# The tail of a filter stage: earlier loads into an idle buffer, and the last chunk's stores on ScalarE's queue

## The chip, the cores and the metric

One core of a Trainium2 chip runs the kernel as one launch. The metric is the time of an execution on the device in microseconds (us), the median over runs. The profile is of one such execution; its span, from the first instruction to the last, is 1531.3 us.

## The reference, cut to what matters

The input is x, eight images of 32 x 32 pixels with 128 channels, so eight sequences of T = 1024 tokens. Three blocks follow one another, each added to the stream: attention over each image, a pair of state-space mixers (one forwards, one backwards), and a spectral filter unit. The change lies in the last one:

```
t = t + _L1_ffn_ref(_ln_t(t), sigma, phi, M_u, M_phi_plus, M_phi_minus, ...)
# _L1_ffn_ref, for the bank that a hard choice picks:
#   U_plus, U_minus = causal convolutions of u with 16 filters phi[:, k] (by FFT)
#   out = sum over k of (U_plus[k] @ Mpp[k] + U_minus[k] @ Mpm[k]) * sigma[k]**0.25
#       + three short autoregressive terms u[t - i] @ Mu[i]
```

The output is the sum of this unit and the stream that came in (the residual). Everything is float32.

## The kernel before, in words

`fast_kernel` computes the filter unit in the frequency domain: forward transforms of the tokens (stage f), a 128 x 128 complex matrix for each frequency applied to the spectra (stage g), and the inverse transform with the residual added (stage i). A general path is kept for inputs that the fast one can't take; it does not run here.

**Stage g, lines 1321 to 1423.** There are NF = 128 frequencies in 16 chunks of FC = 8. The loop at L1406 is a software pipeline over chunks, one step ahead: in the pass for chunk c, TensorE makes the matrices of chunk c + 1 (`matrices`, L1336), ScalarE and VectorE copy them into the tile `gs` (L1347, L1349), and TensorE applies the matrices of chunk c to the spectra `u` (`apply`, L1370). `gs` has two buffers of 64 KB in each partition. In the last pass (chunk 15) no further matrices are made, so the buffer of chunk 14 lies idle from the moment that chunk 14's last `apply` ends. After each quarter of a chunk `gather` (L1385 to L1393) combines the products; after every second quarter, SyncE's queue stores `sums` (256 KB) into the DRAM tensor `yd`, so two stores per chunk. `yd` is indexed by frequency first; the following stage needs frequencies in partitions. That turn of the data is why it goes through DRAM.

**Stage i, lines 1425 to 1468.** The output is made in four pieces (k, h): half k of each sequence, and images h*4 to h*4 + 3. A piece needs its spectra `yt` with the frequency in the partition: two loads (i = 0, 1, the real and imaginary part) of 128 rows x 4 images x 2 KB, 1024 KB each, and its residual `res` from the DRAM tensor `xa`, 1024 KB. VectorE forms `z` from them (four operations, L1444), TensorE multiplies with the inverse transform `inv` (eight matmuls, four outputs of 128 x 512, L1449; the profile shows each float32 matmul as two records), VectorE adds the residual (four operations, L1456), and ScalarE's queue stores the piece, 1024 KB (L1459).

The first piece's spectra live in a tile of their own, `early_yt`, that is filled during stage g: after each chunk, `fetch` (L1397 to L1401) loads the eight rows of the chunk before it, two loads of 64 KB (8 rows x 8 KB). The other three pieces have their `yt` in a pool of two buffers and are loaded whole, after the last chunk. `res` has three buffers, so the fourth residual waits for the first piece's store.

**What sets the order.** TensorE, VectorE, ScalarE and GpSimd execute in the order in which the source is written. The DMAs of SyncE are placed by a scheduler, but each queue then issues strictly in its order: a DMA whose wait is not met holds back everything behind it on that queue. DMAs take eight completion semaphores in turn, and one that takes a semaphore first waits for the DMA that had it before. In effect, a DMA waits for the one eight places ahead of it in the joint order of both queues.

Of the kernel before, what the change touches and what calls it, by code (L numbers as in the profile page):

```python
# [8 lines left out]
F32 = mybir.dt.float32  # L9
AF = mybir.ActivationFunctionType  # L10
ALU = mybir.AluOpType
AX = mybir.AxisListType
PSUM = bass.MemoryType.PSUM

P = 128
B = 8
T = 1024
NT = T // P
C = 128
# [11 lines left out]
NB = 2  # L31
NF = 128
FC = 8
# [11 lines left out]
def fast_kernel(ctx: ExitStack, tc: tile.TileContext, a: dict, out: bass.AP, bad: bass.AP):  # L45
    nc = tc.nc
    x = a["x"]
# [27 lines left out]
    me = dram.tile([P, 2 * KF, P], F32, name="me")  # L75

    ud = dram.tile([NF // FC, P, B, NB, 2, 4, FC], F32, name="ud")
    yd = dram.tile([NF, NB, B, 2, 4, C], F32, name="yd")

    def filled(name, shape, value):  # L80
        t = ctile(shape, name)
# [436 lines left out]
    with ExitStack() as s:  # L518
# [87 lines left out]
        sums = {}  # L606
# [608 lines left out]
    with ExitStack() as s:  # L1215
# [105 lines left out]
        with ExitStack() as s2:  # L1321
# [56 lines left out]
            def gather(c, n, turn, py):  # L1378

                if turn == 0:  # L1380
                    gathered["sums"] = p3.tile([P, 4, C], F32, tag="sums", name=f"sums{c}_{n}")
                    gathered["both"] = p2.tile([P, 2, C], F32, tag="both", name=f"both{c}_{n}")
                sums, both = gathered["sums"], gathered["both"]
                half = p2.tile([P, C], F32, tag="half", name=f"half{c}_{n}_{turn}")
                nc.scalar.copy(half, py[:, 1, :])  # L1385
                nc.vector.tensor_tensor(both[:, turn, :], py[:, 0, :], half, ALU.add)
                nc.vector.tensor_tensor(sums[:, 2 + turn, :], py[:, 0, :], half, ALU.subtract)
                if turn == 0:
                    return
                nc.vector.tensor_tensor(sums[:, 0, :], both[:, 0, :], both[:, 1, :], ALU.add)  # L1390
                nc.vector.tensor_tensor(sums[:, 1, :], both[:, 0, :], both[:, 1, :], ALU.subtract)
                at = c * FC + n * 4
                nc.sync.dma_start(  # L1393
                    yd[at : at + 4].rearrange("f k b i q e -> (f k b i) (q e)"), sums.rearrange("p q e -> p (q e)")
                )

            def fetch(c):  # L1397

                rows = slice(c * FC, (c + 1) * FC)
                for i in range(2):  # L1400
                    nc.sync.dma_start(early_yt[rows, i], yd[rows, 0, 0:4, i])  # L1401

            chunks = NF // FC
            gs, us, gathered = {}, {}, {}
            s2.enter_context(tc.manual_schedule(engines=IN_ORDER))
            for c in range(-1, chunks):  # L1406
# [13 lines left out]
                        gather(c, half, turn, py)  # L1420
                if c > 0:
                    fetch(c - 1)
            fetch(chunks - 1)

        with ExitStack() as s2:
            p2 = s2.enter_context(tc.tile_pool(name="i_2", bufs=2))
            p3 = s2.enter_context(tc.tile_pool(name="i_3", bufs=3))
            ps_o = s2.enter_context(tc.tile_pool(name="i_ps_o", bufs=4, space=PSUM))

            def loaded(k, h):  # L1430

                yt = early_yt
                if k or h:
                    yt = p2.tile([P, 2, 4, 4, C], F32, tag="yt", name=f"yt{k}_{h}")
                    for i in range(2):
                        nc.sync.dma_start(yt[:, i], yd[:, k, h * 4 : h * 4 + 4, i])
                res = p3.tile([P, 4, 4, C], F32, tag="res", name=f"res{k}_{h}")
                nc.sync.dma_start(res, xa[h * 4 : h * 4 + 4, :, NB - 1 - k].rearrange("b p r c -> p b (r c)"))
                return yt, res

            def back(k, h, yt, res):
                z = p2.tile([P, 2, 2, 4, C], F32, tag="z", name=f"z{k}_{h}")
                for r, i, op in ((0, 0, ALU.subtract), (0, 1, ALU.add), (1, 0, ALU.add), (1, 1, ALU.subtract)):
                    nc.vector.tensor_tensor(z[:, r, i], yt[:, i, :, 2, :], yt[:, 1 - i, :, 3, :], op)  # L1444
                blk = NB - 1 - k
                for r in (0, 2, 1, 3):
                    po = ps_o.tile([P, 4, C], F32, tag="o", name=f"pz{k}_{h}_{r}")
                    for i in range(2):
                        nc.tensor.matmul(  # L1449
                            po,  # L1450
                            lhsT=inv[:, r, i, :],
                            rhs=z[:, r // 2, i] if r % 2 else yt[:, i, :, r // 2, :],
                            start=(i == 0),
                            stop=(i == 1),
                        )
                    nc.vector.scalar_tensor_tensor(  # L1456
                        res[:, :, r, :], po, keep[:, blk : blk + 1], res[:, :, r, :], ALU.mult, ALU.add
                    )
                nc.scalar.dma_start(  # L1459
                    out[h * 4 : h * 4 + 4, blk * 512 : (blk + 1) * 512].rearrange("b (p r) c -> p b (r c)", r=4), res  # L1460
                )

            pieces = [(k, h) for k in range(NB) for h in range(2)]
            got = [loaded(*piece) for piece in pieces[:3]]
            for n, piece in enumerate(pieces):
                back(*piece, *got[n])
                if n + 3 < len(pieces):
                    got.append(loaded(*pieces[n + 3]))


@with_exitstack
# [803 lines left out]
```

## Time and profile before

| what | value |
|---|---|
| time, median of 3 runs | 1534.85 us (1531.8 to 1535.4) |
| span of the profiled execution | 1531.3 us |
| busy: TensorE, VectorE, ScalarE, GpSimd | 1438.4, 1152.8, 867.8, 442.4 us |
| mean TensorE clock granted | 0.979 |
| DMA, mean over the span | 58 GB/s (89.05 MB) |
| last chunk's last matmul ends | 1478.9 us |
| first matmul of the inverse transform | 1488.3 us |
| last store of the output issued | 1523.6 us |

The profile gives busy times of the engines, a timeline, the waits with what ended them, and for any stretch the granted clock, the share of time that the 16 DMA engines were busy, and the GB/s that they moved. TensorE is busy for 94% of the span, but that says little on the end of the kernel: the last 52 us, after the last chunk, have a rhythm of their own, and the change touches only these and the few us ahead of them. A name such as SPq or ACTq is the queue of SyncE or ScalarE, where a DMA is issued; the time beside it is that of the issue, not of the transfer.

### The profile page before, as it was taken

How to read it: one execution, taken by the hardware profiler on the slowest of the kernel's cores; microseconds unless marked ns; L12 is line 12 of the kernel's file. 1: busy time of each engine (PE TensorE's matmuls, PEld its weight loads, DVE VectorE, ACT ScalarE, POOL GpSimd, SP SyncE). 2: the span in 40 equal slices, each digit the busy share in tenths (PEclk: the TensorE clock that was granted, in tenths of full speed). 3: DMA queues.
4: the chain of work that ended last, by engine and by line, in shares of the span. 5: the costliest groups of instructions: out<-in, count | busy, mean ns of one | idle time of the engine just before them, and what ended most of it. 6: DMA issues, size and time to landing. Idle time of an engine off the chain costs nothing.

```text
span 1531.3 us, 45713 instructions
## 1 busy us (share of the span) xinstructions
PE 1438.4 (94%) x20118; PEld 879.1 (57%) x20118; DVE 1152.8 (75%) x2314; ACT 867.8 (57%) x1228; POOL 442.4 (29%) x488
## 2 busy tenths in 40 slices
PE   5999999999998899999999999999779999999976
PEld 2323333333334566666665666666569899989962
DVE  6689888778675888888888888887655577777744
ACT  3756666666666465656566666555345455555520
POOL 2336786584201112121111112111166411111100
PEclk9999999999999899999999999999899999999989
DMA  7001111110000011010101010101047622322258
GB/s 187 21 1 35 49 35 37 47 42 8 1 1 13 2 26 31 15 42 15 42 15 42 15 42 15 42 15 42 14 152 219 182 69 70 79 75 74 66 143 304
DMA packets 131960, 89.05 MB, mean 58 GB/s; under 512 B 41480, under 2 KB 114824, under 8 KB 131752
## 3 DMA queue, kind: packets, MB, share of 16 engines
q1 hardware_dynamic: 129640, 81.84, 19.4%
q8 instruction: 160, 2.62, 0.8%
q10 hardware_dynamic: 2112, 4.19, 0.7%
q14 instruction: 48, 0.39, 0.1%
HBM read 44.60 MB, written 33.55 MB: 51 GB/s over the span
## 4 chain that ended last, share of the span: by engine, by line
PE 83%; DVE 5%; ACT 5%; issue 3%; DMA 2%; POOL 1%; ACTq 0%; DVEq 0%; SPq 0%; POOLq 0%
PE pg L1336 9%; PE pt L618 9%; PE py L1370 8%; PE pb L847 7%; PE po L639 7%; PE pd L659 4%; PE sy L1042 4%; PE pz L798 4%; PE pp L798 4%; PE pl L935 4%; PE spo L1072 3%; PE pe L953 3%; PE sb L905 2%; PE pst L973 2%; PE pf L1254 2%
## 5 line engine op out<-in xcount | busy, mean ns | idle before, releaser
L623 ACT ACTIVATE pr<-pt 128x1024 f32<-128x1024 f32 x256 | 248.1, 1021 | 115.1 <-PE pt L618 113.5
L648 DVE TENSOR_TENSOR two<-pr,pr 128x1024 f32<-128x1024 f32 x128 | 162.9, 1314 | 19.5 <-ACT pr L623 18.6
L1349 ACT COPY gs<-pg 128x512 f32<-128x512 f32 x256 | 133.8, 598 | 63.8 <-PE pg L1336 48.8
L1347 DVE COPY gs<-pg 128x512 f32<-128x512 f32 x256 | 159.2, 685 | 13.5 <-PE pg L1336 10.1
L618 PE MATMUL pt<-q,k 32*128 32x512 f32 x1024 | 159.8, 654 | 7.0 <-ACT pr L623 4.5
L1336 PE MATMUL pg<-taps,mst 32*128 32x128 f32 x4096 | 147.5, 280 | 4.8 <-ACT gs L1349 2.2
L1336 PEld LDWEIGHTS pg<-taps,mst 32*128 32x128 f32 x4096 | 134.4, 186 | 18.1 <-issue 13.8
L639 PE MATMUL po<-pr,v 128*32 128x512 f32 x1024 | 140.2, 605 | 0.0
L827 DVE SCALAR_TENSOR_TENSOR xs<-xp,cw,xs 128x1024 f32<-128x1024 f32 x96 | 123.1, 1283 | 7.4 <-ACT xs L819 5.2
L1370 PE MATMUL py<-gs,u 128*32 128x128 f32 (+1 forms) x4096 | 127.8, 277 | 0.0
L1370 PEld LDWEIGHTS py<-gs,u 128*32 128x32 f32 (+1 forms) x4096 | 112.0, 141 | 7.3
L1102 POOL TENSOR_TENSOR rms<-rms_v,mhalf 128x8 f32<-128x8 f32 x16 | 39.2, 2452 | 262.2 <-DVE rms_v L1100 262.2
L847 PE MATMUL pb<-bxt,wbc 128*128 128x512 f32 x256 | 114.2, 598 | 0.3 <-ACT zs L838 0.3
L781 POOL TENSOR_TENSOR dau<-upto,da 128x2048 f32<-128x2048 f32 x16 | 57.9, 3619 | 133.7 <-DVE state L987 133.7
L618 PEld LDWEIGHTS pt<-q,k 32*128 32x128 f32 x1024 | 47.6, 186 | 84.9 <-issue 33.0
L1359 POOL TENSOR_SCALAR u<-u 128x512 f32<-128x512 f32 x16 | 24.1, 1504 | 229.0 <-PE pg L1336 117.7
L990 DVE SCALAR_TENSOR_TENSOR state<-state,dec,pst 128x64 f32<-128x64 f32 x448 | 87.3, 275 | 1.1
L847 PEld LDWEIGHTS pb<-bxt,wbc 128*128 128x128 f32 x256 | 47.1, 189 | 56.0 <-issue 53.8
L639 PEld LDWEIGHTS po<-pr,v 128*32 128x32 f32 x1024 | 28.0, 109 | 88.4 <-issue 84.4
L1042 PEld LDWEIGHTS sy<-lm,xdt 64*64 64x64 f32 x2048 | 58.8, 137 | 29.9 <-DVE ec L1016 15.2
L659 PE MATMUL pd<-two,ones 128*32 128x512 f32 x512 | 73.3, 613 | 0.2
L1042 PE MATMUL sy<-lm,xdt 64*64 64x64 f32 x2048 | 65.5, 226 | 5.5 <-DVE lm L1012 5.5
(272 smaller groups left out, 2846.2 us busy)
## 6 DMA issues: line engine op xcount, KB each, us to landing
ud<-sp SPq DMA_DIRECT2D x8, 1024.0 KB
u<-ud SPq DMA_DIRECT2D x32, 256.0 KB
yd<-sums SPq DMA_DIRECT2D x32, 256.0 KB
moved<-state SPq DMA_DIRECT2D x48, 128.0 KB
yt<-yd SPq DMA_DIRECT2D x6, 1024.0 KB
X<-in_x SPq DMA_DIRECT2D x8, 512.0 KB
part_p<-in_L_ffn_M_phi_plus SPq DMA_DIRECT2D x32, 128.0 KB
part_m<-in_L_ffn_M_phi_minus SPq DMA_DIRECT2D x32, 128.0 KB
```

The costliest lines, as they stand in the source:

```text
L618: nc.tensor.matmul(pt[:, i, :], lhsT=k[rows, j * P : (j + 1) * P], rhs=q[rows, cols], start=True, stop=True)
L623: nc.scalar.activation(pr[:, 2 * g : 2 * g + 2, :].rearrange("p i t -> p (i t)"), pt.rearrange("p i t -> p (i t)"), AF.Exp, scale=SCALE,)
L639: nc.tensor.matmul(po[rows, :], lhsT=vs[b][:, j, rows], rhs=pr[:, h, :], start=(j == 0), stop=(j == NT - 1))
L648: nc.vector.tensor_tensor(two, sums["pr"][:, 2 * g : 2 * g + 2, :], pr[:, 2 * g : 2 * g + 2, :], ALU.add)
L659: nc.tensor.matmul(sums["d"][(2 * g + i) * DH : (2 * g + i + 1) * DH, :], lhsT=ones[:, :DH], rhs=two[:, i, :], start=(j == 1), stop=(j == ...
L827: nc.vector.scalar_tensor_tensor(acc, xp[:, at : at + T], cw[u.d][:, n, i : i + 1], acc, ALU.mult, ALU.add)
L847: nc.tensor.matmul(u.pb[:, i * 512 : (i + 1) * 512], lhsT=wbc[u.d][:, k, :], rhs=xt[:, at : at + 512], start=(k == 0), stop=(k == KC - 1),)
L1042: nc.tensor.matmul(u.py[c][h * HP : (h + 1) * HP, r, j, :], lhsT=left, rhs=right, start=(kind == 0), stop=(kind == 1 or k is None),)
L1336: nc.tensor.matmul(pts[g][:, e, :], lhsT=mst[rows, n * 4 + e, :], rhs=taps[rows, cols].rearrange("p f q m i -> p (f q m i)"), start=True, ...
L1347: nc.vector.tensor_copy(to, frm)
L1349: nc.scalar.copy(to, frm)
L1370: nc.tensor.matmul(py[t * 32 : t * 32 + 32 - 16 * m, q // 2, :], lhsT=u[:, i, m:, :, :, q * FC + f].rearrange("p k b i -> p (k b i)"), rhs ...
```

## The change

It is meant to use the time of the last chunk for the loads of stage i. Almost all rows of `yd` are known by then, and one `gs` buffer is idle.

- The two tensors part: `yd` keeps chunks 0 to 14, and a new DRAM tensor `yl` takes chunk 15. The two stores into `yl` are issued by ScalarE's queue.
- At the end of the pass for chunk 14 the idle `gs` buffer becomes a tile `free` of eight slots of 8 KB in each partition. Six hold the spectra of the second, third and fourth piece, two hold the residuals of the first and second. For each of the six spectra slots SyncE loads rows 0 to 111 (chunks 0 to 13, 896 KB) and rows 112 to 119 (chunk 14, 64 KB) as two DMAs.
- After the last chunk, ScalarE's queue loads rows 120 to 127 of all four pieces from `yl`: eight DMAs of 64 KB.
- When chunk 15's matrices are used up, their buffer becomes a second `free`: two slots for the residuals of the third and fourth piece, two for `z`. No buffer has to be waited for after that.
- Stage i uses the eight PSUM buffers of stage g in place of four of its own, and `z` of the following piece is computed between the two halves of a piece.
- `fetch` stays as it was for chunks 0 to 14: the call for chunk 14 stands in the pass for chunk 15, and so, in the source, after the new loads.

```
-    yd = dram.tile([NF, NB, B, 2, 4, C], F32, name="yd")
+    yd = dram.tile([NF - FC, NB, B, 2, 4, C], F32, name="yd")
+    yl = dram.tile([FC, NB, B, 2, 4, C], F32, name="yl")
...
+                to = yd[at : at + 4] if c + 1 < chunks else yl[n * 4 : n * 4 + 4]
+                (nc.sync if c + 1 < chunks else nc.scalar).dma_start(
+                    to.rearrange("f k b i q e -> (f k b i) (q e)"), sums.rearrange("p q e -> p (q e)")
+                )
+            old, last = (slice(0, NF - 2 * FC), slice(NF - 2 * FC, NF - FC)), slice(NF - FC, NF)
+            def free():
+                t = p2.tile([P, P, C], F32, tag="gs", name="free")
...
                 if c > 0:
                     fetch(c - 1)
-            fetch(chunks - 1)
+                if c == chunks - 2:
+                    room = free()
...
+                    for n in range(4):
+                        k, h = pieces[n]
+                        for i in range(2):
+                            if n:
+                                for rows in old:
+                                    nc.sync.dma_start(yts[n][i][rows], yd[rows, k, h * 4 : h * 4 + 4, i])
+                        if n < 2:
+                            load_residual(k, h, results[n])
+            for n, (k, h) in enumerate(pieces):
+                for i in range(2):
+                    nc.scalar.dma_start(yts[n][i][last], yl[:, k, h * 4 : h * 4 + 4, i])
+            room = free()
+            for n in range(2):
+                results.append(half_piece(room, n))
+                load_residual(*pieces[2 + n], results[2 + n])
+            zs = [half_piece(room, 2 + n).rearrange("p (r i) b c -> p r i b c", r=2) for n in range(2)]
...
+            z = turned_back(0)
+            for n, (k, h) in enumerate(pieces):
+                for r in (0, 2):
+                    back(n, r, z)
+                following = turned_back(n + 1) if n + 1 < len(pieces) else None
+                for r in (1, 3):
+                    back(n, r, z)
+                z = following
```

More of the change, by code (lines that the diff above doesn't have):

```diff
@@ L1392, in gather, with half_piece, load_residual @@
                 at = c * FC + n * 4
+                to = yd[at : at + 4] if c + 1 < chunks else yl[n * 4 : n * 4 + 4]
+                (nc.sync if c + 1 < chunks else nc.scalar).dma_start(
+                    to.rearrange("f k b i q e -> (f k b i) (q e)"), sums.rearrange("p q e -> p (q e)")
+                )
+            chunks = NF // FC
+            old, last = (slice(0, NF - 2 * FC), slice(NF - 2 * FC, NF - FC)), slice(NF - FC, NF)
+            def free():
+                t = p2.tile([P, P, C], F32, tag="gs", name="free")
+                return t.rearrange("p n e -> p (n e)").rearrange("p (k x) -> p k x", k=8)
+            def half_piece(t, k):
+                return t[:, k].rearrange("p (b r c) -> p b r c", b=4, r=4)
+            def load_residual(k, h, res):
                 nc.sync.dma_start(
-                    yd[at : at + 4].rearrange("f k b i q e -> (f k b i) (q e)"), sums.rearrange("p q e -> p (q e)")
+                    res.rearrange("p b r c -> p b (r c)"),
+                    xa[h * 4 : h * 4 + 4, :, NB - 1 - k].rearrange("b p r c -> p b (r c)"),
                 )
@@ L1401, in fetch @@
                     nc.sync.dma_start(early_yt[rows, i], yd[rows, 0, 0:4, i])
-            chunks = NF // FC
             gs, us, gathered = {}, {}, {}
@@ L1422, in fast_kernel @@
                     fetch(c - 1)
-            fetch(chunks - 1)
[L1425 to L1442, printed above, removed]
+                if c == chunks - 2:
+                    room = free()
+                    pieces = [(k, h) for k in range(NB) for h in range(2)]
+                    yts = [[early_yt[:, i] for i in range(2)]]
+                    yts += [[half_piece(room, 2 * n + i) for i in range(2)] for n in range(3)]
+                    results = [half_piece(room, 6 + n) for n in range(2)]
+                    for n in range(4):
[6 more added lines that the diff above has]
+                            load_residual(k, h, results[n])
@@ new lines, in fast_kernel, with turned_back @@
+            for n, (k, h) in enumerate(pieces):
[6 more added lines that the diff above has]
+            zs = [half_piece(room, 2 + n).rearrange("p (r i) b c -> p r i b c", r=2) for n in range(2)]
+            def turned_back(n):
+                y, z = yts[n], zs[n % 2]
@@ L1443, in back @@
                 for r, i, op in ((0, 0, ALU.subtract), (0, 1, ALU.add), (1, 0, ALU.add), (1, 1, ALU.subtract)):
-                    nc.vector.tensor_tensor(z[:, r, i], yt[:, i, :, 2, :], yt[:, 1 - i, :, 3, :], op)
+                    nc.vector.tensor_tensor(z[:, r, i], y[i][:, :, 2, :], y[1 - i][:, :, 3, :], op)
+                return z
+            def back(n, r, z):
+                k, h = pieces[n]
                 blk = NB - 1 - k
[L1446 to L1457, printed above, removed]
-                    )
+                po = ps_g.tile([P, 4, C], F32, tag="g", name=f"pz{n}_{r}")
+                for i in range(2):
+                    nc.tensor.matmul(
+                        po,
+                        lhsT=inv[:, r, i, :],
+                        rhs=z[:, r // 2, i] if r % 2 else yts[n][i][:, :, r // 2, :],
+                        start=(i == 0),
+                        stop=(i == 1),
+                    )
+                to = results[n][:, :, r, :]
+                nc.vector.scalar_tensor_tensor(to, po, keep[:, blk : blk + 1], to, ALU.mult, ALU.add)
@@ L1459, in back @@
+            z = turned_back(0)
[6 more added lines that the diff above has]
+                z = following
+                blk = NB - 1 - k
                 nc.scalar.dma_start(
-                    out[h * 4 : h * 4 + 4, blk * 512 : (blk + 1) * 512].rearrange("b (p r) c -> p b (r c)", r=4), res
-                )
@@ L1463, in fast_kernel @@
[L1463 to L1468, printed above, removed]
+                    out[h * 4 : h * 4 + 4, blk * 512 : (blk + 1) * 512].rearrange("b (p r) c -> p b (r c)", r=4),
+                    results[n].rearrange("p b r c -> p b (r c)"),
+                )
```

## The prediction

> **What bounds the kernel now.** I read the timeline of the last 62 us first, then the waits in it, then busy time and DMA by stretch. The timeline:
>
> ```profile
> 1469.78 9.07 PE L1370 MATMUL py<-gs,u 128*32 128x128 f32 x320
> ...
> 1473.12 0.34 SPq L1393 DMA_DIRECT2D yd<-sums  x1
> ...
> 1480.57 0.37 SPq L1438 DMA_DIRECT2D res<-xa  x1
> 1482.22 0.64 SPq L1401 DMA_DIRECT2D early_yt<-yd  x2
> ...
> 1488.27 6.75 PE L1449 MATMUL pz<-early_yt,inv 128*128 128x512 f32 x8 [9.43 <-DMA res<-xa]
> ...
> 1516.39 1.98 PE L1449 MATMUL pz<-yt,inv 128*128 128x512 f32 x4 [2.04 <-DMA yt<-yd]
> ...
> 1523.57 0.38 ACTq L1459 DMA_DIRECT2D out<-res  x1
> ```
>
> The first row holds five times 64 matmuls: chunk 14's last quarter and all of chunk 15. So chunk 14's buffer is idle from about 1469.8 + 9.07/5 = 1471.6, only 7.2 us before the chunks end at 1478.9. From there TensorE waits 9.4 us until 1488.27, for the last eight rows of `early_yt`: the load named as its releaser (`res`) is not among what it needs, `early_yt` is. I call the start of the first piece S; here S = 1488.3. From S to the end it is 1531.3 - 1488.3 = 43.0 us. The waits in the tail:
>
> ```profile
> PE pz L1449 <- DMA res<-xa: 9.4, 1, 9.4
> DVE z L1444 <- DMA early_yt<-yd: 9.1, 1, 9.1
> ...
> DVE res L1456 <- DMA res<-xa: 1.8, 1, 1.8
> ```
>
> What S to the end costs without waits for data: eight half-clock records until the next group starts at 1494.86 take 6.6 us; 56 more at 3.43 us for eight (1494.86 to 1498.29) take 24.0, with 0.2 for the last one to drain; the last addition 0.75 and two short gaps 0.1; from the issue of the last store to the end 1531.3 - 1523.6 = 7.7. Sum 39.3. The measured 43.0 has 3.7 more, the waits for the fourth piece's `yt` and residual. So loads that lie ready would save 3.7 us after S. The rest is decided by S itself, and S by DMA:
>
> ```profile
> 1471.70:1480.60 8.90, 7.15 (x260) 6.85 (x252) 3.65 (x16) 1.34 (x5) 0.00 (x0) 1.00 0.23 77
> 1480.60:1485.50 4.90, 0.00 (x0) 0.00 (x0) 0.00 (x0) 0.00 (x0) 0.00 (x0) 0.87 0.90 293
> 1485.50:1488.50 3.00, 0.23 (x1) 0.26 (x2) 0.00 (x0) 0.00 (x0) 0.00 (x0) 0.50 1.04 110
> 1488.50:1514.00 25.50, 25.30 (x52) 10.59 (x52) 16.05 (x24) 0.00 (x0) 0.00 (x0) 0.88 1.05 395
> ```
>
> The last three columns are TensorE's clock, DMA share and GB/s. While chunk 15 is multiplied DMA is 23% busy; that is the room the change wants. From 1488.5 on DMA is full at 395 GB/s, and computing runs beside it: piece 1 starts when 128 KB have come, the other 9 MB come while it works. The third row is odd: DMA is as busy as ever but moves only 110 GB/s, for 3.0 us. Those are the us in which the two eight-row loads of `early_yt` (128 KB) go through.
>
> [...]after 1503 stores from ScalarE's queue and loads from SyncE's together still make about 400 GB/s. So ScalarE's queue adds no bandwidth. [...]of 3.0 us x 110 GB/s = 330 KB, the pair is 131 KB; the other 199 KB would take 0.5 us at 395, so the pair cost 2.5 us, 1.25 each in place of 0.17 at full rate.
>
> **The change, part by part.** The listing of the changed kernel's order shows where SyncE's queue puts what:
>
> ```
> L1412 free<-xa 128x4x512              residual of piece 1
> L1396 yd<-sums_1 128x512              chunk 14's second store
> L1454 free<-yd 112x4x512, 8x4x512     twice, piece 2
> L1412 free<-xa 128x4x512              residual of piece 2
> L1454 free<-yd 112x4x512, 8x4x512     four times, pieces 3 and 4
> L1421 early_yt<-yd 8x4x512            twice: chunk 14's rows of piece 1
> L1412 free<-xa 128x4x512              twice: residuals of pieces 3 and 4
> ```
>
> This is the point on which all hangs. The rows 112 to 119 of `early_yt` are fetched at 1475.8 and 1477.0 before; now they stand behind every load of pieces 2 to 4, and TensorE and VectorE can't start piece 1 without them. So S is the time at which nearly everything has been loaded, and loads and computing, side by side before, come one after the other.
>
> S, step by step. The first new load can go at 1471.7; before, the store issued at 1480.14 showed traffic 0.9 us later, so data flows from 1472.6. At 395 GB/s, 1024 KB take 2.65 us.
> 1. Wide loads and stores ahead: two residuals 2048 KB, chunk 14's store 256, six loads of 896 KB 5376, two stores of chunk 15 512: 8192 KB, 21.2 us. I take 112 rows at the rate of 128; no row shows them[...].
> 2. Eight-row loads on SyncE's queue: six and the two of `early_yt`, at 1.25 each 10.0 us (1.4 at full rate).
> 3. Eight-row loads on ScalarE's queue: eight; from 0.17 to 1.25 each. [...]I take 0.7, 5.6 us (1.4 to 10).
> 4. From the last data to the waiting engine 0.5 us: the loads that wait for the store of 1480.14 issue at 1482.22, so of these 2.1 us 0.9 are the start, 0.7 its 256 KB, and 0.5 the landing.
>
> S = 1472.6 + 21.2 + 10.0 + 5.6 + 0.5 = 1509.9.
>
> Waits that the change adds: SyncE's first eight-row load waits for chunk 14's store to land, and behind it stand all later loads; one load and the store are then in flight, so DMA is not idle. A later one waits, through its semaphore, for chunk 15's second store, about 1483; several MB are queued then. ScalarE's store of chunk 15's first half waits for VectorE's sums at 1476.6, ahead of a copy (`half`) that can't start before 1477.2 anyway: nothing. The eight loads behind the second store wait for its landing, about 1483, and are through long before S.
>
> After S: all data but the last two residuals (5.3 us) is there, so 39.3 us. Moving `z` ahead of the second half of a piece and eight PSUM buffers cost nothing: VectorE needs 2.5 + 4 x 0.75 = 5.5 us a piece beside TensorE's 6.9. TensorE idles longer, so its half-clock start stays.
>
> Span: 1509.9 + 39.3 = 1549.2, 17.9 more than 1531.3; time 1534.85 + 17.9 = 1553. S breaks even at 1531.3 - 39.3 = 1492.0.
>
> **Rivals.**
> - *Clean loads*: an eight-row load costs only its bytes. 21.2 + 1.4 + 1.4 in steps 1 to 3 gives S = 1497.1, span 1536.4, time 1540. For it: alone, in the pass of a chunk, such loads harm nobody. Against: the 110 GB/s.
> - *Everything blocks*: ScalarE's loads cost 1.25 each too (4.4 more) and 112 rows run 1.25 times as long (3.6): S = 1517.9, time 1561.
> - *Hidden as meant*: the last rows of `early_yt` get through early, so S stays at about 1488 or comes to 1486, and the 3.7 us of waits go: time 1529 to 1531, faster. For it: data for pieces 2 to 4 begins to flow 9 us earlier, and the fourth piece's wait is real. Against: the order of the queue. In the 13.5 us from 1472.6 to 1486 DMA can move 5.3 MB at 395 GB/s, and 9.4 MB stand before `early_yt`.
>
> **How the numbers follow.** Main case 0.62, clean loads 0.16, everything blocks 0.16, hidden 0.06. Predicted 1553. The range goes from the clean case, 1540, to the blocking one with a little for 112 rows worse than taken, 1564. Even the clean case is 0.33% slower, so slower takes all but the last rival and a sliver: slower 0.92, same 0.03, faster 0.05.
>
> **What would show it.** In the profile after: `early_yt<-yd` as the last load but two on SyncE's queue, issued around 1500 or later; TensorE idle about 30 us in one piece before L1478; nearly no idle from then on; S to the end 39 us; stretches between 1478 and S with a DMA share near 1 but well under 395 GB/s. If S is under 1492 the central step, that piece 1 waits for the end of the queue, is wrong. If S is near 1497 the price of eight-row loads is wrong; near 1518 or above, that of 112 rows or ScalarE's loads.

## The result

The changed kernel takes 1558.64 us (1557.74 to 1559.98), the kernel before, timed beside it, 1534.07. The ratio is 1.0162, with a 95% interval of 1.0145 to 1.018: slower by 24.6 us. The forecast was 1553.0, slower by 17.9 us, with a range of 1540 to 1564.

To compare profiles that are shifted against each other, I count from R, the start of chunk 14's last quarter, with which the long row of TensorE begins, and again call the start of the first piece S. All numbers "R + ..." below are differences of two times in one profile.

| | R | S - R | S to end | R to end |
|---|---|---|---|---|
| before | 1469.78 | 18.5 | 43.0 | 61.5 |
| after | 1471.52 | 49.6 | 37.0 | 86.6 |

Up to R the two profiles differ by 1.7 us, in work that the change doesn't touch. The loss is all in S - R, which grew by 31.1 us; the second part got 6.0 shorter.

### The profile after

The timeline of TensorE in the tail (start, length, engine, line, operation; in brackets the idle time ahead and what ended it):

```profile
1471.52 6.45 PE L1372 MATMUL py<-gs,u 128*32 128x128 f32 x215
1481.29 4.65 PE L1372 MATMUL py<-gs,u 128*16 128x128 f32 x105 [3.33 <-issue]
1521.10 5.80 PE L1478 MATMUL pz<-early_yt,inv 128*128 128x512 f32 x8 [35.16 <-DMA early_yt<-yd]
1526.74 24.20 PE L1478 MATMUL pz<-free,inv 128*128 128x512 f32 x56
```

Two things are to be seen. The third row is what the prediction spoke of: TensorE idles 35.2 us for the rows of `early_yt`, and then runs through the other pieces without a gap. The first two rows are new: the 320 matmuls that made one row before are broken after 215 of them, and TensorE stands still for 3.3 us with "issue" as the reason, that is, with nothing that the profile shows to wait for.

SyncE's and ScalarE's queues in the same time:

```profile
1475.23 7.29 SPq L1454 DMA_DIRECT2D free<-yd  x4
1484.55 0.38 SPq L1412 DMA_DIRECT2D free<-xa  x1
1485.90 22.18 SPq L1454 DMA_DIRECT2D free<-yd  x8
1512.13 0.61 SPq L1421 DMA_DIRECT2D early_yt<-yd  x2
1513.33 0.94 SPq L1412 DMA_DIRECT2D free<-xa  x2
```

```profile
1487.25 0.34 ACTq L1396 DMA_DIRECT2D yl<-sums  x1
1495.16 0.92 ACTq L1459 DMA_DIRECT2D early_yt<-yl  x2
1496.11 10.15 ACTq L1459 DMA_DIRECT2D free<-yl  x6
```

Chunk 14's rows of `early_yt` are issued at 1512.13, behind the twelve loads of pieces 2 to 4, as the order of the queue had it. The eight loads from `yl` can't start before 1495.16, because the second store into `yl` was issued at 1487.25 and took 7.9 us to land. The chain of waits that ends last runs through just these:

```profile
1487.25 7.89 DMA yl<-sums
...
1495.80 6.65 DMA early_yt<-yl
...
1502.48 9.63 DMA free<-yl
...
1512.13 8.72 DMA early_yt<-yd
...
1521.10 29.85 PE pz L1478 x64
```

Between the first and the last of these DMAs the chain has no engine's work at all. Its first link is a need: `early_yt<-yl` reads what the store wrote. The next two are a completion semaphore. In the profile before, 345 DMAs use eight of these, and in 327 of 337 repeats the same one comes back with the eighth DMA after. In this trace the three loads shown use one and the same in turn, so `early_yt<-yd`, which needs nothing of `free<-yl`, waits for it all the same. SyncE's queue shows the same from its side (us in total, times, longest):

```profile
SPq L1454 <- DMA free<-yl: 9.2, 1, 9.2
SPq L1454 <- DMA yl<-sums: 8.9, 1, 8.9
...
SPq L1421 <- DMA free<-yl: 4.0, 1, 4.0
```

And the stretches, of which the last three columns are TensorE's clock, the DMA share and GB/s:

```profile
1474.50:1521.10 46.60, 8.12 (x234) 7.07 (x226) 3.08 (x14) 1.07 (x4) 0.00 (x0) 0.64 0.95 221
1493.50:1497.50 4.00, 0.00 (x0) 0.00 (x0) 0.00 (x0) 0.00 (x0) 0.00 (x0) 0.50 0.58 153
1505.50:1509.50 4.00, 0.00 (x0) 0.00 (x0) 0.00 (x0) 0.00 (x0) 0.00 (x0) 0.50 0.67 155
1513.50:1515.50 2.00, 0.00 (x0) 0.00 (x0) 0.00 (x0) 0.00 (x0) 0.00 (x0) 0.50 0.73 189
```

From the first load to S the DMA engines are busy nearly all the time, but move 221 GB/s, where the kernel before moved 395 beside its pieces. In three stretches, 10 us together, a part of them stands idle: 4 x 0.42 + 4 x 0.33 + 2 x 0.27 = 3.5 us of full idleness.

### The profile page after: what moved, and what is told of

The parts are those of the page before. It is cut to its first block, busy times and chain, and to the rows that moved or that the text cites. A ratio compares the mean times of both kernels' runs of the same rounds, so it can differ in the third digit from the quotient of the medians.

```text
span 1558.1 us, 45725 instructions
## 1 busy us (share of the span) xinstructions
PE 1439.8 (92%) x20118; PEld 879.6 (56%) x20118; DVE 1152.8 (74%) x2314; ACT 868.2 (56%) x1228; POOL 442.8 (28%) x488
## 3 DMA queue, kind: packets, MB, share of 16 engines
q1 hardware_dynamic: 129128, 80.79, 19.7%
```

## The experiments

My theory after the result: S is late because chunk 14's rows of `early_yt` stand last in SyncE's queue; the loads ahead of them are slow because each eight-row load costs much more than its bytes. Rivals: the loads of 112 rows are the slow ones; ScalarE's queue is slow by itself; TensorE's pause is what delays all. S and the pieces' stalls tell them apart.

### The rows of early_yt first in the queue

```
-                if c > 0:
+                if 0 < c < chunks - 1:
                     fetch(c - 1)
                 if c == chunks - 2:
+                    fetch(c)
                     room = free()
```

> The changed kernel with the two eight-row loads of chunk 14 into early_yt issued ahead of the loads of pieces 2 to 4; nothing else differs. Theory A (piece 1 waits for the end of SyncE's queue): piece 1 then starts when its rows 120 to 127 land, which took until 1502 in the changed kernel, so S falls from 1521 to about 1500, computing runs beside the rest of the loads, and the time falls by 12 to 20 us, to about 1541. Theory B (the transfers as a whole set the end, wherever the queue puts these two): S may fall, but pieces 2 to 4 wait as long, and the time falls by less than 4 us.

Measured: 1547.05 us, ratio 1.0062 (1.0046 to 1.0078), span 1545.4. S - R fell from 49.6 to 22.3 us, so the place in the queue is shown to be what makes S late. Theory A holds: by the ratios the time fell by 15.3 us (12 to 20 expected). But of the 27.3 us that S - R lost only 15.0 remain from R to the end (86.6 and 71.6):

```profile
1496.03 2.05 PE L1478 MATMUL pz<-early_yt,inv 128*128 128x512 f32 x2 [10.43 <-DMA early_yt<-yl]
1499.13 5.46 PE L1478 MATMUL pz<-early_yt,inv 128*128 128x512 f32 x6 [1.05 <-DMA free<-xa]
1504.38 18.62 PE L1478 MATMUL pz<-free,inv 128*128 128x512 f32 x42
1524.62 2.84 PE L1478 MATMUL pz<-free,inv 128*128 128x512 f32 x6 [1.63 <-SPq L2277]
1531.69 5.40 PE L1478 MATMUL pz<-free,inv 128*128 128x512 f32 x8 [4.22 <-DVE free L1470]
```

The first piece starts early, and the others then run into loads that are not there yet; S to the end is 49.4 us. From 1496 to 1530 DMA moves 260 GB/s at a share of 1.00. So there are two causes: the order, and loads that stay slow wherever they stand.

### The same, with all loads held until the last chunk's sums are made

The block of loads stands behind the loop over the chunks in this version; the lines below leave that out.

```
+            for slot in [s for n in range(1, 4) for s in yts[n]] + results:
+                nc.vector.memset(slot[:, 0, 0, 0:1], 0.0)
```

> As the run with the early fetch, and in addition a one-element memset by VectorE in each slot of the idle buffer holds all loads into it until the last chunk's sums are made. Theory A (loads during the last chunk hurt: TensorE's pause of 3.3 us in chunk 15 and the late landing of the last stores are due to them): the pause is gone, the last store lands 2 us after its issue and not 8, and the time is no more than 3 us longer than that of the early fetch alone, though all loads start 8 us later. Theory B (the early start is worth its 8 us of DMA, and the pause has another cause): the time is 6 to 9 us longer than that of the early fetch alone, and the pause stays.

Measured: 1548.16 us, ratio 1.0073 (1.0058 to 1.0089). TensorE's row is whole again, with no pause:

```profile
1473.81 9.10 PE L1372 MATMUL py<-gs,u 128*32 128x128 f32 x320
1497.21 5.83 PE L1479 MATMUL pz<-early_yt,inv 128*128 128x512 f32 x8 [14.30 <-DMA free<-yd]
```

Held by some 7 us, the loads cost only 1.1 us more than in the version before (at most 3 expected). So starting them early brought almost nothing, even with the right order. The pause goes with loads that run during chunk 15, and since the time without it is no better, the pause isn't what delays all. One part of theory A failed: the load that waits for the last store is issued 5.6 us after it (1484.23, 1489.79) and not 2, because by then the held loads are under way.

### Without the eight-row loads of pieces 2 to 4

The six spectra slots are filled by loads of 128 rows with other data; the twelve eight-row loads are left out.

```
-                                for rows in old:
-                                    nc.sync.dma_start(yts[n][i][rows], yd[rows, k, h * 4 : h * 4 + 4, i])
+                                nc.sync.dma_start(
+                                    yts[n][i].rearrange("p b r c -> p b (r c)"),
+                                    xd[h * 4 : h * 4 + 4, i * 512 : (i + 1) * 512].rearrange("b (p r) c -> p b (r c)", r=4),
+                                )
...
-            for n, (k, h) in enumerate(pieces):
+            for n, (k, h) in enumerate(pieces[:1]):
```

> The changed kernel with the 12 eight-row loads of pieces 2 to 4 left out, and 128 rows of another tensor of the same row length loaded whole in place of the 112: the spectra of pieces 2 to 4 are not the right data, so it is for the time alone. The queue's order is otherwise the same, early_yt's rows still stand behind. Theory A (eight-row loads are what makes the loading slow): 1474.5 + 21.9 us for eight wide loads and a store + 1.3 for the last stores + four eight-row loads at 1.25 + 0.5 gives S about 1503 in place of 1521, time about 1541. Theory B (the wide loads with 112 rows, or the chain of semaphores, are what is slow): with these gone too the fall is the same in B's first form, but the packets of the wide loads in the changed kernel would then be slow also where no eight-row load runs; in its second form S stays above 1512.

Measured: 1551.12 us, ratio 1.0088 (1.0072 to 1.0105); S - R is 36.0 us in place of 49.6. Expected was S at about 1503 on the changed kernel's clock, which is 31.5 us after R, so it came 4.5 us later than I had worked out.

```profile
1486.00:1500.00 14.00, 4.35 (x97) 3.87 (x89) 1.38 (x6) 0.53 (x2) 0.00 (x0) 0.64 1.04 393
1500.00:1512.00 12.00, 0.00 (x0) 0.00 (x0) 0.00 (x0) 0.00 (x0) 0.00 (x0) 0.50 1.06 241
```

While the loads of 128 rows run it is 393 GB/s, as good as the 395 of the kernel before. In the last 12 us, with the four remaining eight-row loads and the two last residuals, it is 241. This looked like a proof that the eight-row loads alone are slow, at 13.6 us for twelve. It wasn't, since two things were changed at once: the twelve loads went, and 112 rows became 128.

### The loads of 112 rows by themselves

The lower rows of pieces 2 to 4 get other data, by one DMA at the end of the queue.

```
-                                for rows in old:
-                                    nc.sync.dma_start(yts[n][i][rows], yd[rows, k, h * 4 : h * 4 + 4, i])
+                                rows = old[0]
+                                nc.sync.dma_start(yts[n][i][rows], yd[rows, k, h * 4 : h * 4 + 4, i])
...
-            for n, (k, h) in enumerate(pieces):
+            for n, (k, h) in enumerate(pieces[:1]):
...
+            nc.sync.dma_start(
+                early_room[NF - 2 * FC :, 0:6],
+                xd.rearrange("b t c -> (b t) c")[0 : 96 * 16].rearrange("(p k r) c -> p k (r c)", p=16, k=6),
+            )
```

> The changed kernel without the twelve eight-row loads of pieces 2 to 4: the six loads of 112 rows stay as they are, and the sixteen rows below them are filled by one DMA with other data at the very end of SyncE's queue, so the outputs of pieces 2 to 4 are not the right ones. Against the version with six loads of 128 rows (first piece at 36.0 us after R, the start of chunk 14's last quarter) it moves 768 KB less ahead of the first piece, 2.0 us at 395 GB/s. My theory (all of the excess lies with eight-row loads; 112 rows run at the full rate): the first piece starts at R + 33.5 to 34.5, and the stretches of wide loads show 380 to 400 GB/s. Rival (112 rows [...]run 1.25 times as long, 3.4 us): first piece at R + 37 to 38, and the stretches of wide loads show 300 to 330 GB/s.

Measured: 1559.81 us, ratio 1.0164 (1.0135 to 1.0194), S - R = 39.0 us; after S it waits long for the DMA that fills the lower rows, so the time itself says nothing here. S is 3.0 us later than with 128 rows, though 768 KB less went ahead of it. At 395 GB/s these are 2.0 us, so by S the 112 rows cost 5.0 us, or 5.9 if it is counted that the version with 128 rows had moved 330 KB more of the last two residuals by then.

```profile
1486.00:1500.00 14.00, 0.30 (x9) 0.03 (x1) 0.89 (x4) 0.27 (x1) 0.00 (x0) 0.60 1.05 279
1496.00:1498.00 2.00, 0.00 (x0) 0.00 (x0) 0.00 (x0) 0.00 (x0) 0.00 (x0) 0.50 1.06 253
1498.00:1500.00 2.00, 0.00 (x0) 0.00 (x0) 0.00 (x0) 0.00 (x0) 0.00 (x0) 0.50 1.07 255
```

The same stretch that moved 393 GB/s with 128 rows moves 279 with 112, at the same DMA share. It holds a residual of 128 rows and a store besides; in its last 4 us, when these have landed and only loads of 112 rows are moved, it is 253 to 255. With the 279 of the whole stretch, six loads of 896 KB, 5.5 million bytes, take 19.7 us in place of 14.0 at 393: 5.7 us more, in keeping with S. My theory expected 380 to 400 GB/s and fell; the rival was right and still too mild, with 300 to 330. The loads of 128 rows read another tensor, but that is not the reason: the version with whole rows, below, reads 128 rows of `yd` itself, at 391 GB/s. Why 112 rows are slow no run shows.

For the twelve eight-row loads there remain 49.6 - 39.0 = 10.6 us, and in that difference lie the 3.5 us of idleness, which this version does not have (its share from 1474.5 to S is 1.04). That leaves about 7 us, 0.6 each, as against 0.17 for their bytes. This is what is left over, not a measured price: part of the idleness could belong to these loads too.

### Whole rows

The spectra of pieces 2 to 4 are loaded whole after the last chunk, into the idle buffer; only the first two residuals are loaded early. `yd` is one tensor again, and all is on SyncE's queue.

```
-                    for n in range(4):
...
-                                for rows in old:
-                                    nc.sync.dma_start(yts[n][i][rows], yd[rows, k, h * 4 : h * 4 + 4, i])
-                        if n < 2:
-                            load_residual(k, h, results[n])
+                    for n in range(2):
+                        load_residual(*pieces[n], results[n])
+            fetch(chunks - 1)
+            for n in range(1, 4):
+                for i in range(2):
+                    nc.sync.dma_start(yts[n][i], yd[:, k, h * 4 : h * 4 + 4, i])
```

> What the change could keep without its split loads: one DRAM tensor, stores by SyncE, the residuals of pieces 1 and 2 in the idle buffer during the last chunk, early_yt's rows first after it, then the spectra of pieces 2 to 4 as whole 128-row loads, no buffer waited for, z and PSUM as in the change. Theory A (order and split rows did the harm, the idle buffer itself is worth the 3.7 us of waits and up to 3 us of S): 1526 to 1531, 3 to 8 us faster than before. Theory B (loads during the last chunk cost TensorE its instructions whatever they are): a pause in chunk 15 of 2 to 4 us eats it, 1531 to 1535.

Measured: 1536.26 us, ratio 1.0002 (0.9989 to 1.0015), no different from before, as theory B had it. R to the end is 61.9 us as against 86.6, and no piece waits in TensorE:

```profile
1472.45 6.39 PE L1371 MATMUL py<-gs,u 128*32 128x128 f32 x215
1482.15 4.71 PE L1371 MATMUL py<-gs,u 128*16 128x128 f32 x105 [3.32 <-issue]
1494.02 6.17 PE L1471 MATMUL pz<-early_yt,inv 128*128 128x512 f32 x8 [7.16 <-DMA early_yt<-yd]
1500.03 24.20 PE L1471 MATMUL pz<-free,inv 128*128 128x512 f32 x56
```

From 1494 to 1514 DMA moves 391 GB/s. The buffers, the PSUM and the order of `z` are those of the changed kernel, so none of these did harm that shows. The loss came with the split loads and their place in the queues. But two early residuals are enough for the pause of TensorE, 3.3 us. S - R is 21.6 in place of 18.5, which eats what is saved after S, where it takes 40.3 us in place of 43.0.

### The last chunk's stores on ScalarE's queue, alone

```
-                nc.sync.dma_start(
+                (nc.sync if c + 1 < chunks else nc.scalar).dma_start(
```

> The kernel before with one part of the change alone: the last chunk's two stores go to a DRAM tensor of their own and are issued by ScalarE's queue; the two eight-row loads of early_yt for chunk 15 stay on SyncE's queue, and nothing is loaded early. My theory: the 7.9 us that the last store took to land in the changed kernel [...]not from ScalarE's queue, so here it lands about 2.1 us after its issue as before, the first piece starts about 18.5 us after the start of chunk 14's last quarter, and the time is that of before within 1.5 us. Rival: ScalarE's queue is itself slow to start a transfer (2.3 to 4.4 us were seen for its first packets in the changed kernel); then the store lands 4 us or later after its issue, the first piece starts 2 us or more later, and the time is 2 us or more above before.

The kernel that ran has only this edit: its stores still go into `yd`, not into a tensor of their own.

Measured: 1534.85 us, ratio 0.9984 (0.9971 to 0.9998). The interval only just leaves out 1, and S - R (19.0 us, 18.5 before) shows no gain, so I count it as no difference.

```profile
1485.47 0.37 ACTq L1393 DMA_DIRECT2D yd<-sums  x1
1487.93 0.62 SPq L1401 DMA_DIRECT2D early_yt<-yd  x2
```

The loads behind the last store are issued 2.5 us after it, nearly the 2.1 of before. So ScalarE's queue isn't slow in itself. The 7.9 us of the changed kernel come with the traffic that the store meets there. The changed kernel's DMA packets say how: none of the store's is moved in the first 4.6 us after the issue (0.9 us here), while SyncE's loads keep the DMA share at 1.03 and 270 GB/s; then they are moved within 2.2 us, beside those of the loads (1.1 us here).

### All of it on SyncE's queue

```
-                (nc.sync if c + 1 < chunks else nc.scalar).dma_start(
+                nc.sync.dma_start(
...
-                    nc.scalar.dma_start(yts[n][i][last], yl[:, k, h * 4 : h * 4 + 4, i])
+                    nc.sync.dma_start(yts[n][i][last], yl[:, k, h * 4 : h * 4 + 4, i])
```

> The changed kernel with all that it put on ScalarE's queue (chunk 15's two stores, the eight eight-row loads behind them) on SyncE's queue instead; there the stores stand behind the loads of pieces 2 to 4, then the rows of early_yt, then the other six eight-row loads. Six of the sixteen eight-row loads so fall behind the first piece's last load. My theory: an eight-row load costs about 1.2 us whichever queue issues it, so the first piece starts 3.1 + 21.2 (8192 KB wide) + 10 x 1.25 + 2 (landing of the store) + 0.5 = 39.3 us after the start of chunk 14's last quarter in place of 49.6, and with 38 us from there to the end the time is about 1552. Rival: the loads of ScalarE's queue run beside those of SyncE's and cost little; then nothing is won by moving them, the first piece starts 48 us or later, and the time is 1558 or more.

Measured: 1557.68 us, ratio 1.0144 (1.0129 to 1.016), S - R = 43.9 us. Neither expectation holds: S came 5.7 us earlier than in the changed kernel, so the rival's 48 or more is out, but 4.6 later than I had worked out, and the time is nearly that of the changed kernel. The chain shows what I had left out:

```profile
1481.28 15.17 DMA free<-yd
...
1496.95 13.88 DMA yl<-sums
...
1510.88 3.27 DMA early_yt<-yl
```

The last store takes 13.9 us to land. I had allowed 2. It is issued behind the loads of pieces 2 to 4, and lands as the traffic ends: from 1496.5 to 1506.5 the DMA share is 1.05 to 1.07, at 195 to 251 GB/s, and in the two stretches of 2 us after that 0.70 and 0.46. By these rates about 3 MB are moved between its issue and its landing. Once the store has landed, at 1510.8, only eight-row loads are under way until the last residuals are issued at 1516.7. Up to 1513 the rate is uneven; then it is steady:

```profile
1514.50:1516.50 2.00, 2.00 (x3) 0.87 (x4) 1.09 (x2) 0.00 (x0) 0.00 (x0) 0.50 0.54 53
```

At 53 GB/s, with a DMA share of 0.54, 64 KB take 1.24 us. That is the price of 1.25 which the prediction took from the odd row. Where other loads run beside them, less is left over for each: 0.6 us by the version with 112 rows alone.

### One early residual: what the pause depends on

The version with whole rows suggested one that might win: load a residual early, but not so that TensorE pauses. Four arrangements, all with whole rows and with one early residual instead of two. First, held until the sums of chunk 15's first half are made, by a one-element VectorE operation on its slot:

```
+                    if c == chunks - 1 and n == 1:
+                        fetch(c - 1)
+                        nc.vector.memset(results[0][:, 0, 0, 0:1], 0.0)
+                        load_residual(*pieces[0], results[0])
```

> Whole 128-row spectra after the last chunk as in the version with whole rows, but only one residual is loaded early (the first piece's), and it is held until the sums of chunk 15's first half are made, about 6.5 us after the start of chunk 14's last quarter, by when TensorE's last instruction block for the chunk has come; the order after it is the second residual, chunk 15's rows of early_yt, then the other pieces' loads. My theory (TensorE's pause of 2.5 to 3.3 us in chunk 15 is an instruction fetch behind the early loads): no pause, the first piece starts 18.0 to 18.5 us after the start of chunk 14's last quarter, 40 to 41 us from there to the end since 1024 KB less must come in between, time 2 to 3.5 us under before. Rival (any large load during chunk 15 makes TensorE pause[...]): a pause of 1 us or more in TensorE's row of chunk 15, first piece at 20 us or later, time at or above that of before.

Second, the same residual not held:

```
                     results = [half_piece(room, 6 + n) for n in range(2)]
+                    load_residual(*pieces[0], results[0])
```

> As the version with one held residual, except that this residual's load is not held: it is issued as soon as chunk 14's buffer is idle, 1.9 us after the start of chunk 14's last quarter, so 1024 KB and a store of 256 KB go through at about 3.1 to 6.3 us. My theory: the instruction block that comes at 3.6 us in the kernel before waits for what is queued ahead of it, here half of what it is in the version with two early residuals (there it came at 7.4 us and TensorE paused 3.3 us from 6.4 us on); so it comes at about 5.5 to 6.5 us and TensorE pauses between 0 and 1.5 us. Time then between that of the held version and 1.5 us above it. Rival (the pause is a fixed cost of any early load): 3 us of pause as with two residuals, and 3 us above the held version.

Measured: held 1534.12 us, ratio 0.9989 (0.9976 to 1.0002), no pause; not held 1536.45 us, ratio 0.9998 (0.9987 to 1.001), with the full pause of 3.3 us.

```profile
1469.74 9.58 PE L1371 MATMUL py<-gs,u 128*32 128x128 f32 x320
1491.87 5.31 PE L1473 MATMUL pz<-early_yt,inv 128*128 128x512 f32 x8 [12.55 <-DMA early_yt<-yd]
```

```profile
1475.90 6.42 PE L1371 MATMUL py<-gs,u 128*32 128x128 f32 x215
1485.63 3.15 PE L1371 MATMUL py<-gs,u 128*16 128x128 f32 x105 [3.31 <-issue]
```

The first expectation held for the pause and failed for S, which is at R + 22.1 (18.0 to 18.5 expected): the residual was issued only at R + 9.2, since two loads stood ahead of it, and the last store lay behind it and landed 4.6 us after its issue. The second failed in its size: I had expected 0 to 1.5 us of pause for half the data.

The DMA records fit both. The profile shows single packets of 16 KB on a DMA queue of the kind "instruction" (q8): the execution before has 160 of them and 40,236 matmuls and weight loads of TensorE, about 250 for each packet. That they bring TensorE's instructions is my reading of this count and of the times that follow. Before, one of them is moved from R + 3.6 to R + 4.5. In the version with the residual at once, loads fill the engines from R + 3.2 to R + 7.2 (1024 KB and a store of 256), and this packet is moved from R + 7.4 to R + 8.35, just after. I had taken the data to be gone at R + 6.3. TensorE stops after the same 215 matmuls in every kernel that has a pause, at R + 6.2 to 6.5, and goes on 0.9 to 1.5 us after the packet is there.

The third and fourth arrangement test that. In the third the residual is released by the sums of the first quarter, and so runs between two packets; in the fourth it is split in two halves of 512 KB, one at once, one held.

```
-                    if c == chunks - 1 and n == 1:
-                        fetch(c - 1)
+                    if c == chunks - 1 and n == 0:
                         nc.vector.memset(results[0][:, 0, 0, 0:1], 0.0)
                         load_residual(*pieces[0], results[0])
+                        fetch(c - 1)
```

> As the version with one held residual, but the load is released earlier, when the sums of the first quarter of chunk 15 are made (about 4.5 us after the start R of chunk 14's last quarter), and stands ahead of chunk 14's rows of early_yt on SyncE's queue; so it goes through at R + 5.6 to R + 8.3, behind the instruction block that comes at R + 3.6 and ahead of chunk 15's last store at R + 10.3. My theory: in the version before, the residual was issued only at R + 9.15 and chunk 15's last store lay behind it (landed 4.6 us after its issue in place of 2.1), which lost 2.5 us or more of the gain; here no pause of TensorE, the first piece starts at R + 18.5 to 19.5, 38.6 us from there to the end, R to the end 57 to 58 us in place of 61.5, time 3.5 to 4.5 us under before. Rival: the two eight-row loads, now behind the residual, hold the last store back just as long; then the first piece starts at R + 20.5 or later and the time is within 2 us of before.

```
                     results = [half_piece(room, 6 + n) for n in range(2)]
+                    load_half(*pieces[0], results[0], 0)
...
-                        load_residual(*pieces[0], results[0])
+                        load_half(*pieces[0], results[0], 1)
```

> As the version with the residual between, but the residual is loaded in two halves of 512 KB: the first at once when chunk 14's buffer is idle (R + 1.9), the second held until the sums of chunk 15's first quarter are made. My theory: an instruction block waits for just the data that is queued ahead of it; with 512 KB and a store of 256 KB ahead (768 KB, 1.9 us from R + 3.2 on) it comes at about R + 5.3, before TensorE needs it at R + 6.45, so there is no pause (0.3 us at most), where 1280 KB gave 3.3 us. The time is then that of the version with the residual between or up to 1 us less, 3.5 to 5 us under before. Rival (a fixed cost of any early load at this place): a pause of 3 us, and 2 us or more above the version with the residual between.

Measured: between 1535.87 us, ratio 0.9993 (0.9984 to 1.0002); halves 1535.68 us, ratio 0.9996 (0.9986 to 1.0007).

```profile
1475.52 9.05 PE L1371 MATMUL py<-gs,u 128*32 128x128 f32 x320
1494.66 5.52 PE L1473 MATMUL pz<-early_yt,inv 128*128 128x512 f32 x8 [10.10 <-DMA early_yt<-yd]
...
1519.79 6.28 PE L1473 MATMUL pz<-free,inv 128*128 128x512 f32 x14 [1.58 <-DMA free<-yd]
```

```profile
1472.25 6.20 PE L1371 MATMUL py<-gs,u 128*32 128x128 f32 x215
1480.37 3.15 PE L1371 MATMUL py<-gs,u 128*16 128x128 f32 x105 [1.92 <-issue]
```

With the residual between the packets there is no pause, and S is at R + 19.1, both as expected; but S to the end is 40.8 us and not 38.6, because now the fourth piece's second spectra load comes late (the wait of 1.6 us). With halves the pause is 1.9 us. I had expected none, with the packet at R + 5.3; it was there at R + 6.7. So the rival, a fixed cost, is out, but my sum of queued bytes was too short again.

Over all kernels the pause follows the end of that one packet, to some tenths of a us:

| kernel | packet moved by, R + | pause, us |
|---|---|---|
| before | 4.5 | none |
| held until the last chunk's sums | 4.6 | none |
| residual between | 4.6 | none |
| held residual | 5.2 | none (row 0.5 us longer) |
| stores on ScalarE's queue | 5.3 | 0.3 |
| half residuals | 6.7 | 1.9 |
| all on SyncE's queue | 7.0 | 1.7 |
| rows of early_yt first | 7.4 | 2.5 |
| without eight-row loads | 8.2 | 3.05 |
| after; whole rows; residual at once; 112 rows | 8.3 to 8.35 | 3.3 |

What sets the packet's own time is not settled by this. The changed kernel and the one with all on SyncE's queue have issued the same loads and store by R + 4, and yet the packet is moved by R + 8.3 in one and R + 7.0 in the other.

As time, the four arrangements lie 0.2 to 1.1 thousandths under before (0.9998, 0.9989, 0.9993, 0.9996), each with 1 in its interval. None is shown to beat the kernel before.

## Why the prediction was right

Direction and central mechanism were right, and the time is in the range. But the size was nearer to the rival "everything blocks": moved by the 1.7 us of R, the main case puts S at 1511.6 and the rival at 1519.6, and 1521.1 was measured. That is the sign which the prediction named for a wrong price of the 112 rows or of ScalarE's loads. The profile's span is 1558.1, the predicted one 1549.2. The difference of 8.9 us is 1.7 from ahead of R, 9.5 in S - R (49.6 where the steps give 1509.9 - 1469.8 = 40.1), and -2.3 in S to the end. By its own steps:

- **The central step**, that piece 1 waits for the end of SyncE's queue, is shown: `early_yt<-yd` is issued at 1512.13, TensorE idles 35 us in one piece, and putting only these loads first takes 27.3 us off S - R. But the prediction left open what that would bring in time. It brings 15 us, little more than half, since the slow loads then hold up pieces 2 to 4.
- **Step 1, wide transfers at 21.2 us.** This is the term that was mis-sized most. "I take 112 rows at the rate of 128" is wrong: 279 and not 393 GB/s, 5.7 us more (5.0 to 5.9 by S). The prediction said that no row shows them and took the cheap end. The dear end, the 1.25 times of "everything blocks", was an assumption of mine that rested on no trace; it was too low even so, 3.6 us (a quarter of the 13.9 us for six loads is 3.5).
- **Steps 2 and 3, 10.0 + 5.6 = 15.6 us for sixteen eight-row loads.** Subtracting everything else from the 49.6 us (3.1 to the first data, 21.2, 5.7, 2.2 and 3.5 from the next points, 0.5 landing) leaves 13.4, so 0.8 each on average. So far as this remainder can be trusted, the sum was right to 2 us. The price of 1.25 is borne out where eight-row loads run alone (53 GB/s), and the odd row comes again just ahead of S: from 1517.5 to 1519.5 the share is 1.04 and DMA moves 104 GB/s, while the last eight-row loads go through. The 0.7 us each for ScalarE's loads was my choice between 0.17 and 1.25; whether they ran partly beside the others can't be told from these runs.
- **That only what stands ahead of `early_yt` in the queue comes before S**, as the steps' sum takes it. It wasn't so: from 1474.5 to 1521.1, 221 GB/s x 46.6 us = 10,060 KB were moved; the chain's own are 8192 + 16 x 64 = 9216. The 840 KB more, 2.2 us, are nearly all of the last two residuals, which stood behind `early_yt` in the queue but went partly beside it: by the DMA packets 1272 of their 2048 KB were left at S. The prediction let them come wholly after S. That this made S later by the 2.2 us no run tests.
- **The waits that the change adds, put at nothing**, are the step that failed in kind. The second store was to land at about 1483. Chunk 15 ended later because of the pause, the store was issued at 1487.25 and took 7.9 us; ScalarE's eight loads were issued from 1495 to 1506 and not "through long before S"; and SyncE's queue waited 8.9 us for the store and, through the shared semaphores, 9.2 and 4.0 us for loads of ScalarE's queue. The 3.5 us of idle DMA fall into the time of these waits; that the waits cost just these is argued, no run has the waits alone taken away. I had thought of each wait as hidden by the megabytes queued at the time, not of waits in both queues that release each other by turns.
- **The sum of these:** 5.7 + 2.2 + 3.5 - 2.2, and 0.3 for the first data, is the 9.5 us. The small loads are what is left over in it, so the sum is no test of them.
- **S to the end, 39.3.** Measured 37.0: the first eight matmuls take 5.6 us in place of 6.6 (granted clock 0.62 and 0.53), and from the last store's issue to the end it is 1.3 less. TensorE waited for no data, as forecast.
- **The moved `z` and the eight PSUM buffers at no cost**: shown by the version with whole rows, which has both and equals the kernel before.
- **The rivals.** "Clean loads" is refuted by the stretches at 150 to 280 GB/s. "Everything blocks" was nearest in S and right on 112 rows, though too mild (1.25 times as long; 393 / 279 is 1.41). Its other part, all sixteen small loads at 1.25 us, would be 20.0 us where 13.4 are left over, so its nearness is partly luck. "Hidden as meant" is excluded by the order of the queue, with `early_yt<-yd` issued at 1512.13.
- **Two readings that don't hold.** In the kernel before, piece 1 needed more than that "128 KB have come": its residual, issued ahead of them at 1480.57, went through first, and 293 GB/s x 4.9 us are 1.4 MB. And the 9.4 MB "before `early_yt`" count ScalarE's loads and `early_yt` itself; ahead of it on SyncE's queue were 8.3 MB. Neither changes the argument, 8.3 MB being still more than the 5.3 that could be moved.

What stays open: whether the pause costs the changed kernel anything by itself (the version with 112 rows has the same pause and no idle DMA; no kernel was run that has the change without the pause and is otherwise the same), why 112 rows are slow, and what sets the time of the instruction packet.

## What to carry to other kernels

Before splitting a load so that part of it can go early, look where the last part that the next stage needs stands in its queue, and at what rate the parts run: 112 + 8 + 8 rows were far slower here than 128 at once (279 GB/s for the 112 rows and 0.6 to 1.25 us for an eight-row load, as against 393 GB/s), and that cost more than the head start of some 9 us was worth. Loads that filled an idle time here also held back what came next on the DMA engines: the last store landed after 7.9 us in place of 2.1, and an instruction packet was moved by R + 8.3 in place of R + 4.5. So let them end before the next short transfer on the critical path starts. And when an early load brings S forward, check the later pieces for data before counting the gain.

## What I had not expected

- TensorE stopped beside early loads with nothing shown that it waits for: where a 16 KB instruction packet was moved late behind them, by R + 6.7 to 8.35, the stop was 1.7 to 3.3 us, shown under "issue" (0.3 us in the one version with a stop and no early load). In the kernel before, the packet was moved by R + 4.5 and TensorE didn't stop; with 768 to 1280 KB of loads and a store ahead of it, it did. That TensorE had run out of instructions is how I read it.
- Loads of 112 rows x 8 KB are moved at 253 to 255 GB/s where nothing else runs (279 with a residual and a store among them), those of 128 rows at 393, all with the DMA share above 1. The share of busy time alone doesn't tell a slow transfer from a good one; the GB/s do.
- A store of 256 KB that lands 2.1 us after its issue on quiet engines took 7.9 us beside the full queue of SyncE and 13.9 us at the end of it.
